# Cross attention and FFN on one core: beginning a pair's accumulator one pair earlier, and moving the last token tile of z behind the FFN's second inner product

## The chip, the core and the metric

The kernel runs on one core of a Trainium2 chip. The metric is the device time of one execution in microseconds (us). The engines are TensorE (PE; PEld is its weight load, which runs beside the matmuls), VectorE (DVE), ScalarE (ACT), GpSimd (POOL) and SyncE (SP, which here only issues DMAs). Matrix products accumulate in PSUM, which has eight banks of 512 f32 per partition.

## The reference, cut to what matters

```python
def fake_quant(x, scale, zp):
    q = jnp.clip(jnp.round(x / s + z), 0., 255.)
    return (q - z) * s

# x: (2, 1024, 2048), ctx: (2, 2048, 2048), all f32
x = x + matmul(fake_quant(layernorm(x), s1, z1), fake_quant(ctx, s2, z2))
z = layernorm(x)
x = x + z @ kernel + bias
      + einsum("bor,btr->bto", B_eff, einsum("bri,bti->btr", A_eff, z))   # gated LoRA
      + einsum("or,btr->bto", B_shared, einsum("ri,bti->btr", A_shared, z))
```

There are two batches of 1024 tokens. A_eff and B_eff are sums over 16 LoRAs of rank 32, weighted by the gates.

## The kernel before

**Cross attention.** The layer-normed x is rounded to uint8 and centred to bf16 integers, eight token tiles of 128 for each batch. A tile (class XTile, L366 to L434) takes statistics on VectorE (L383), a square root on ScalarE (L341), factors on VectorE (up to L402), the rounded row (L409, on ScalarE for all of batch 1), two halves of centring with a sum on ScalarE (L412), two times eight transposes on TensorE (L423) into PSUM, the copy into c1T (L428) and the row's zero point term r_s (L432). Two tiles are a group g = 0..3. The context is quantised by ScalarE (L458) and centred by VectorE (L464), in column blocks n = 0..3 of 512, two of which are held at a time. For each block, `column_term` adds up the columns on TensorE (pcp, L486), copies (L499), takes the mean (pc, L505) and makes the column's zero point term `colt[n]` (L511).

The product of a group and a column block is a `Pair`: a PSUM accumulator `pa` of two banks, one for each token tile j, from three rotating tags. `begin(j)` (L526, ScalarE) writes colt + r_s into half j; `products` (L530) adds 16 matmuls of 128x512 in bf16 to a half; `end` (L547, VectorE) adds the scaled accumulator to y, the running output in SBUF; `stats` (L551) takes the statistics of z. Dependences between instructions on PSUM are kept for a whole tile, so both halves of `pa` count as one. `xattn_pair` (L555 to L563) does begin(0), products of half 0, begin(1), products of half 1, and has the begins in high priority.

Batch 0 starts with a list of steps in an order written by hand (`entry`), which does columns 0 and 1 and the pair (2,0) without `xattn_pair`. Batch 1 has its first tiles prepared during the FFN of batch 0; then columns 0 and 1 go by groups, tiles 4 to 7 being prepared among them (`prep_x`, L1039), and columns 2 and 3 go as in batch 0. Beside the pairs run the LoRA steps: weighted sums of A (pg_a, L574), their transposes (pga, L600), and weighted sums of B (pg_b, L574), which are stored to DRAM (bd).

**z.** `prep_z` (L622) normalises a token tile in two halves on VectorE (L628) into a work buffer wk, transposes it in four groups of four (ptz, L632), and ScalarE copies each (L633). `group_z` does it for the two tiles of a group and stores them to DRAM (zs, issued on ScalarE's queue, L639) for the later outer products. `lora_ax` (L642) multiplies z by LoRA-A (px, L648; axT, L656). These run during column 3: z of group g-1 follows the pair (3, g).

**FFN.** The matmul with the kernel matrix uses a two-level scheme of Strassen's kind: 7 outer products (index o), each of 7 inner products (s, chains u, v, w). `product` (L828) is four f32 matmuls of 128x512, each in two passes, for each of two token tiles; `spread` (L852, VectorE) adds an accumulator to the places of y. Sums of operands (`comb`, L771, and `block`, L762) run on VectorE for the weights' side b and on GpSimd for the z side a; the operands are loaded on SP's queue (L746, L752). `Delta` (L658) holds two PSUM banks and in steps after some products adds bias and LoRA-B times axT (pl, L694; L705).

**Order.** All instructions are put in order ahead of time by a scheduler, engine by engine, from the order in which the program emits them, the priorities and its own estimate of when each is ready. Buffers come from pools (`take`, `give`); a buffer taken again waits for its last reader. The z transposes, the transposes of x, the column sums, px and the LoRA sums share PSUM buffers (ps_m). Before the change, the operands of the first outer product and the z tiles were emitted like this (L1103 to L1109):

```python
group_z(b, 3, wk, zqs[3])      # both tiles, then four stores
big.give(wk)
first.block("b21")
first.comb("t2", "b22", "t1", ALU.subtract)
first.comb("s1", "a21", "a22", ALU.add)
first.comb("s2", "s1", "a11", ALU.subtract)
lora_ax(b, 1, [zqs[2], zqs[3]])
```

and then `ffn`, with `delta = Delta(b)` ahead of its loops.

Of the kernel before, what the change touches and what calls it, by code (L numbers as in the profile page):

```python
# [15 lines left out]
ALU = mybir.AluOpType  # L16
# [82 lines left out]
def tile_quant_xattn_then_lora_ffn(  # L99
# [17 lines left out]
    nc = tc.nc  # L117
    B, S, D = x.shape
    KT = D // P
    MT = S // P  # L120
# [6 lines left out]
    GPB = GB // B  # L127
    GT = B * S // GB
    MG = GT // P
# [422 lines left out]
                    st2[:, self.g * MG + j, self.n, :], y[self.g][:, j, ds(self.n * NB, NB)]  # L552
                )

    def xattn_pair(b, n, g, c1T, c2):  # L555
        p = Pair(b, n, g, c1T, c2)
        for j in range(MG):
            with tc.high_priority():
                p.begin(j)
            p.products(j, range(KT))  # L560
        summed = p.end()
        p.stats()
        return summed  # L563
# [289 lines left out]
            if done:  # L853
                nc.scalar.dma_start(out=out[b, ds(g * GT, GT), cols].rearrange("(j p) n -> p j n", p=P), in_=yp)

    def ffn(b, ops, meanwhile):

        delta = Delta(b)
        for o in range(NO):
            nxt = Operands(b, o + 1) if o + 1 < NO else None  # L860
            chains = {}
            for s in range(len(INNER)):
                product(b, o, s, ops, chains)
                if s in OWN:
                    OWN[s](ops)
                if nxt and s in AHEAD:
                    AHEAD[s](nxt)
                spread(b, o, s, chains)
                if s in (1, 4):
                    delta.step()  # L870
                added = line.last
                if nxt:
                    for name in BLOCKS.get(s, ()):
                        nxt.block(name)
                for name in DROP.get(s, ()):
                    ops.drop(name)
                if nxt:
                    for name in BEGIN.get(s, ()):
                        nxt.load(name)
                with tc.issue_after(added):  # L880
                    meanwhile(o, s)
            ops = nxt
# [20 lines left out]
    wk = big.take()  # L903
    c2b = {}
    c2 = {}
# [4 lines left out]
    def close_c2(n):  # L910
        for t in c2b.pop(n):
            big.give(t)
# [107 lines left out]
    for b in range(B):  # L1020
        if b == 0:
            open_c2(0)
            open_c2(1)
            with in_order(mybir.EngineType.DVE, mybir.EngineType.Activation, mybir.EngineType.PE):
                opened, begun = entry()
            next_block(1)
            with tc.issue_after(last_of[mybir.EngineType.DVE]):
                for p in begun.values():
                    p.stats()
        else:  # L1030
            gate_matrix(b)
            opened = xattn_pair(b, 0, 0, c1T, c2[0])
            xattn_pair(b, 0, 1, c1T, c2[0])
            for g in range(2):
                xattn_pair(b, 1, g, c1T, c2[1])
            for g in range(2, GPB):
                for m in range(g * MG, (g + 1) * MG):
                    with tc.issue_after(opened.ins):
                        prep_x(b, m, c1T, wk)  # L1039
                for n in range(2):  # L1040
                    xattn_pair(b, n, g, c1T, c2[n])
                    if g + 1 == GPB:
                        next_block(n)
                        if n == 0:
                            for r in range(NR):
                                quantise(c2[2], r)
                                if r % 4 == 3:
                                    lora_a_step(b, r // 4)
                            column_term(b, 2, c2[2])
        if b == 0:  # L1050
            for pr in range(GPB // 2):
                nc.sync.dma_start(out=acat[:, :, 3 * pr + 1, :], in_=a_sh)
            for bb in range(B):
                for g in range(GPB):
                    nc.sync.dma_start(out=bd[bb][g, 1 - g % 2], in_=b_sh)
        for g in range(GPB):
            if (b, g) != (0, 0):
                xattn_pair(b, 2, g, c1T, c2[2])
            for r in {0: range(3), 1: range(3, 6), 2: range(6, 8), 3: ()}[g]:
                quantise(c2[3], r)  # L1060
            if 1 <= g <= 2:
                lora_a_step(b, g + 1)
            if g == 2:
                column_term(b, 3, c2[3])
        lora_b_step(b, 0)
        close_c2(2)
        bp.give(colt.pop(2))
        first = Operands(b, 0)
        first.load("b11")
        zqs = {}  # L1070
        for g in range(GPB):
            xattn_pair(b, 3, g, c1T, c2[3])
            big.give(c1T_bufs[g])
            if g == 0:
                first.block("b11")
                first.load("b12")
            elif g == 1:
                first.block("b12")
                first.comb("t1", "b12", "b11", ALU.subtract)
            elif g == 2:  # L1080
                first.load("b22")
            if g < 3:
                lora_b_step(b, g + 1)
            if g > 0:
                zqs[g - 1] = [lit.take() for _ in range(4)]
                group_z(b, g - 1, wk, zqs[g - 1])
            if g == 2:

                lora_ax(b, 0, [zqs[0], zqs[1]])
                for i in range(2):  # L1090
                    for j in range(2):
                        to = lit.take() if i == 0 else zqs[i][j]
                        nc.vector.tensor_add(to, zqs[i][j], zqs[i][2 + j])
                        first.t[f"a{i + 1}{j + 1}"] = to
                for t in (*zqs[0], *zqs[1][2:]):
                    lit.give(t)
        close_c2(3)
        bp.give(colt.pop(3))
        first.block("b22")
        z3 = [big.take() for _ in range(2)]  # L1100
        zqs[3] = [t[:, :, ds(h * GT, GT)] for t in z3 for h in range(2)]
        first.load("b21")
        group_z(b, 3, wk, zqs[3])  # L1103
        big.give(wk)
        first.block("b21")
        first.comb("t2", "b22", "t1", ALU.subtract)
        first.comb("s1", "a21", "a22", ALU.add)
        first.comb("s2", "s1", "a11", ALU.subtract)
        lora_ax(b, 1, [zqs[2], zqs[3]])  # L1109
        for t in zqs[2]:  # L1110
            lit.give(t)
        for t in z3:
            big.give(t)

        state = {"x": 0}

        def meanwhile(o, s):

            if b + 1 == B:
                return  # L1120
            nb = b + 1
            if o < NO - 1:

                for half, m in LOAD_X.get((o, s), ()):
                    load_x(nb, m, slice(half * H, (half + 1) * H))
                return
            if s == 0:
                open_c2(0)
                state["wk"] = big.take()
                state["c1b"] = []  # L1130
                batch[0] = nb
                load_next()
            else:
                load_next()
            if s == 1:
                state["c1b"].append(big.take())
            if s == 3:
                state["c1b"].append(big.take())
            state["c1T"] = [bf(t, GT) for t in state["c1b"]]
            for half, m in LOAD_X.get((o, s), ()):  # L1140
                load_x(nb, m, slice(half * H, (half + 1) * H))
            if s < 4:
                for r in range(2 * s, 2 * s + 2):
                    quantise(c2[0], r)
            if 1 <= s <= 4:
                prep_x(nb, s - 1, state["c1T"], state["wk"])
            if s == 3:
                column_term(nb, 0, c2[0])
                c2b[1] = [big.take()]
                c2[1] = [bf(c2b[1][0], NB)]  # L1150
            if s == 4:
                for r in range(2):
                    quantise(c2[1], r)
                c2b[1].append(big.take())
                c2[1].append(bf(c2b[1][1], NB))
            if s == 5:
                for r in range(2, 5):
                    quantise(c2[1], r)
            if s == len(INNER) - 1:
                for r in range(5, NR):  # L1160
                    quantise(c2[1], r)
                column_term(nb, 1, c2[1])
                state["c1b"] += [big.take() for _ in range(2)]
                state["c1T"] = [bf(t, GT) for t in state["c1b"]]
                for m in range(4, MT):
                    load_x(nb, m, slice(H, D))

        ffn(b, first, meanwhile)
        if b + 1 < B:
            c1T_bufs, c1T, wk = state["c1b"], state["c1T"], state["wk"]  # L1170

# [52 lines left out]
```

## Time and profile before

| | us |
|---|---|
| median of 3 runs | 1082.38 (1082.28 to 1082.62) |
| the profiled execution, its own time | 1082.56 |
| its span | 1080.8 |
| first z transpose of the last z tile of batch 0 | 195.30 |
| first px matmul of the second half, batch 0 / batch 1 | 202.56 / 729.38 |
| first z transpose of batch 1 | 676.35 |

The span runs from the first to the last instruction of the profiled execution; 1.76 us of its time lie outside. Times in the trace count from the span's start. A line of a timeline has the start, the length, the engine, the line of the code, the operation, output <- inputs by their names with sizes, the number of instructions taken together (x16), and in brackets how long the engine had been idle before, and what released it. Matmuls overlap one another, so their distance from start to start says more than their length: 0.2155 us for one in `products`, 0.429 for one of the two passes of an f32 matmul in the FFN, 0.109 for a z transpose, 0.055 for a transpose of x. "Waits" lists for a line of an engine the instructions it waited for, with total time, number and the longest.

### The profile page before, as it was taken

Reading aid. Unit: us, or ns where it says so; the run is one execution under the profiler, and the core shown is the slowest. Engines: PE = TensorE matmul, PEld = TensorE weight load, DVE = VectorE, ACT = ScalarE, POOL = GpSimd, SP = SyncE. Lnnn points to the kernel's source line nnn. Section 1 sums busy time; section 2 is a strip of 40 time slices with the busy share of each in tenths; the row PEclk is TensorE's granted clock in tenths of the full one; section 3 lists DMA queues with packets and bytes.
Section 4 is the critical chain, followed back from the end, with each engine's and each line's share of the span. In section 5 each row is a group of like instructions: output and inputs, shape, how many; then the busy total and the mean of one; then the engine's idle time right before and its main releaser. Section 6 shows DMA issues by size and latency. Waiting matters only on the chain.

```text
span 1080.8 us, 10609 instructions
## 1 busy us (share of the span) xinstructions
PE 1054.6 (98%) x3932; PEld 489.8 (45%) x3932; DVE 766.6 (71%) x949; ACT 247.4 (23%) x351; POOL 253.8 (23%) x104
## 2 busy tenths in 40 slices
PE   5999999999999999999999999999999999999998
PEld 2443345544444444444444444554444444444443
DVE  7986867578877676677859655674969667756851
ACT  5866133210000000001675741331000000000000
POOL 0000003032435302533000000032244531253600
PEclk9999999999999999999999999999999999999999
DMA  9979645788798476699673292559889874748611
GB/s 341 381 196 308 190 176 190 256 316 295 263 339 324 160 264 217 191 372 321 230 246 119 98 266 103 198 210 360 294 269 297 288 269 148 264 146 301 214 39 58
DMA packets 119228, 257.15 MB, mean 238 GB/s; under 512 B 11272, under 2 KB 15496, under 8 KB 118152
## 3 DMA queue, kind: packets, MB, share of 16 engines
q1 hardware_dynamic: 98688, 215.05, 58.4%
q10 hardware_dynamic: 20168, 40.38, 10.7%
q0 software_dynamic: 320, 1.05, 0.4%
q8 instruction: 31, 0.51, 0.2%
q14 instruction: 21, 0.17, 0.1%
HBM read 220.79 MB, written 37.75 MB: 239 GB/s over the span
## 4 chain that ended last, share of the span: by engine, by line
PE 83%; DVE 8%; DMA 4%; ACT 3%; issue 1%; SPq 0%; ACTq 0%
PE fu L828 34%; PE fv L828 17%; PE pa L530 12%; PE fw L828 9%; PE pl L694 3%; PE px L648 3%; PE ptz L632 2%; DMA lit<-in_ctx_dram 2%; DVE st L551 2%; DVE st L383 1%; ACT q2b L458 1%; DVE y L547 1%; ACT big L412 1%; DVE big L771 1%; PE pg_b L574 1%
## 5 line engine op out<-in xcount | busy, mean ns | idle before, releaser
L828 PE MATMUL fu<-big,lit 128*128 128x512 f32 x896 | 395.3, 593 | 0.0
L828 PEld LDWEIGHTS fu<-big,lit 128*128 128x128 f32 x896 | 168.6, 190 | 206.3 <-issue 204.9
L530 PE MATMUL pa<-big,big 128*128 128x512 bf16 x1024 | 237.1, 381 | 7.3 <-ACT pa L526 3.4
L771 POOL TENSOR_TENSOR lit<-lit,lit 128x1024 f32<-128x1024 f32 x56 | 164.7, 2950 | 189.7 <-PE fw L828 74.6
L828 PE MATMUL fv<-big,lit 128*128 128x512 f32 x448 | 197.9, 594 | 0.0
L771 DVE TENSOR_TENSOR big<-big,big 128x2048 f32<-128x2048 f32 x56 | 164.4, 2935 | 0.7
L530 PEld LDWEIGHTS <-big 128*128 128x128 bf16 x1024 | 97.1, 98 | 136.3 <-issue 29.6
L762 POOL TENSOR_TENSOR lit<-lit,lit 128x1024 f32<-128x1024 f32 x32 | 85.7, 2677 | 256.4 <-DMA lit<-zs 230.4
L852 DVE TENSOR_TENSOR y<-y,fu 128x1024 f32<-128x1024 f32 x92 | 108.5, 1215 | 40.6 <-PE fu L828 40.2
L828 PEld LDWEIGHTS fv<-big,lit 128*128 128x128 f32 x448 | 84.3, 190 | 105.0 <-issue 104.7
L458 ACT ACTIVATE q2b<-lit,sc,inv 128x1024 int16<-128x1024 f32 x64 | 76.4, 1232 | 163.7 <-DMA lit<-in_ctx_dram 147.1
L852 DVE TENSOR_TENSOR y<-y,fv 128x1024 f32<-128x1024 f32 x48 | 56.8, 1218 | 78.8 <-PE fv L828 78.8
L762 DVE TENSOR_TENSOR big<-big,big 128x2048 f32<-128x2048 f32 x40 | 101.8, 2546 | 0.0
L828 PE MATMUL fw<-big,lit 128*128 128x512 f32 x224 | 99.4, 592 | 0.0
L683 ACT COPY pl<-bias 128x1024 f32<-128x1024 f32 x16 | 16.3, 1018 | 294.1 <-DVE y L705 258.1
L679 POOL DMA_DIRECT2D bp<-bd x4 | 2.6, 660 | 344.3 <-DMA bd<-q2b 166.3
L852 DVE TENSOR_TENSOR y<-y,fw 128x1024 f32<-128x1024 f32 x24 | 28.4, 1218 | 53.9 <-PE fw L828 53.9
L828 PEld LDWEIGHTS fw<-big,lit 128*128 128x128 f32 x224 | 42.1, 190 | 50.7 <-issue 50.7
L547 DVE SCALAR_TENSOR_TENSOR y<-pa,k_s,y 128x1024 f32<-128x1024 f32 x32 | 41.0, 1280 | 32.2 <-PE pa L530 32.1
L526 ACT ACTIVATE pa<-bp,r_s 128x512 f32<-128x512 f32 x58 | 39.0, 685 | 87.0 <-PE pa L530 57.1
L705 DVE TENSOR_TENSOR y<-pl,y 128x512 f32<-128x512 f32 x64 | 39.8, 679 | 17.5 <-PE pl L694 17.2
L383 DVE BATCH_NORM_STATS2 st<-y 128x6 f32<-128x512 f32 x64 | 41.4, 679 | 5.7 <-DMA y<-in_x_dram 5.6
(93 smaller groups left out, 629.6 us busy)
## 6 DMA issues: line engine op xcount, KB each, us to landing
big<-in_w_dram SPq DMA_DIRECT2D x96, 1024.0 KB
lit<-zs SPq DMA_DIRECT2D x80, 512.0 KB
lit<-in_ctx_dram SPq DMA_DIRECT2D x64, 512.0 KB
out_dram<-y ACTq DMA_DIRECT2D x30, 512.0 KB
zs<-lit ACTq DMA_DIRECT2D x24, 512.0 KB
lit<-in_lora_a_dram SPq DMA_DIRECT2D x32, 256.0 KB
lit<-in_lora_bt_dram SPq DMA_DIRECT2D x32, 256.0 KB
y<-in_x_dram SPq DMA_DIRECT2D x16, 512.0 KB
```

The costliest lines, as they stand in the source:

```text
L383: nc.vector.bn_stats(st1[:, self.m, n, :], self.y[:, ds(n * NB, NB)])
L458: nc.scalar.activation(qi, t, AF.Relu, bias=z2, scale=inv2)
L526: nc.scalar.activation(self.pa[:, j, :], colt[self.n], AF.Identity, bias=r_s[:, m : m + 1])
L530: nc.tensor.matmul(self.pa[:, j, :], self.c1T[:, k, ds(j * P, P)], self.c2[k // 8][:, k % 8, :], start=not self.begun[j], stop=(k == KT - ...
L547: return nc.vector.scalar_tensor_tensor(yp, self.pa, s12, yp, ALU.mult, ALU.add)
L648: nc.tensor.matmul(px[i * 2 * R : (i + 1) * 2 * R, :], acat[:, k, ds(3 * pr + i, 2), :].rearrange("p s r -> p (s r)"), zqs[i][k // KQ][:, ...
L694: nc.tensor.matmul(pl[j][i][:, half], axT[rows, pr, ds(j * P, P)], bt[rows, half], start=False, stop=True, skip_group_check=True,)
L705: line(nc.vector.tensor_add(yb, pl[j][i], yb))
L762: line(eng.tensor_tensor(got[0], got[0], got[1], ALU.add if terms[1][2] > 0 else ALU.subtract))
L771: line(eng.tensor_tensor(out_t, at[p], at[q], op))
L828: nc.tensor.matmul(ps[m], at[:, k, ds(m * P, P)], bt[:, k, :], start=(opens and k == 0), stop=(ends and k == KQ - 1), skip_group_check=True,)
L852: line(nc.vector.tensor_tensor(yp, yp, whole[chain], op))
```

## The change

`xattn_pair` takes the next pair as `then`. It begins both halves of the next pair, in high priority, ahead of the present pair's products, and a pair that is not yet begun has both halves begun in front of its products. In columns 2 and 3 the next pair is given; for the four calls of batch 1's columns 0 and 1 it isn't. The loads of the first outer product's operands move: b11 and b12 ahead of the loop over column 3, b22 and b21 in its first two rounds, and the sum t1 into its third. The last token tile of z (`MT - 1`), the stores of its group, the second `lora_ax` and the construction of `Delta` move into `ffn`, behind the products (0,0) and (0,1), which are emitted together.

```diff
-    def xattn_pair(b, n, g, c1T, c2):
-        p = Pair(b, n, g, c1T, c2)
+    ready = {}
+
+    def begin_pair(b, n, g, c1T, c2):
+        p = ready[b, n, g] = Pair(b, n, g, c1T, c2)
+        with tc.high_priority():
+            for j in range(MG):
+                p.begin(j)
+
+    def xattn_pair(b, n, g, c1T, c2, then=None):
+        if (b, n, g) not in ready:
+            begin_pair(b, n, g, c1T, c2)
+        p = ready.pop((b, n, g))
+        if then:
+            begin_pair(b, *then)
         for j in range(MG):
-            with tc.high_priority():
-                p.begin(j)
             p.products(j, range(KT))
...
-    def ffn(b, ops, meanwhile):
-
-        delta = Delta(b)
+    def ffn(b, ops, meanwhile, last_z):
+
         for o in range(NO):
...
             for s in range(len(INNER)):
-                product(b, o, s, ops, chains)
+                if (o, s) != (0, 1):
+                    product(b, o, s, ops, chains)
+                if (o, s) == (0, 0):
+                    product(b, o, 1, ops, chains)
+                    last_z()
+                    delta = Delta(b)
...
-                xattn_pair(b, 2, g, c1T, c2[2])
+                xattn_pair(b, 2, g, c1T, c2[2], (2, g + 1, c1T, c2[2]) if g + 1 < GPB else (3, 0, c1T, c2[3]))
...
-        first.load("b11")
+        for name in ("b11", "b12"):
+            first.load(name)
+            first.block(name)
...
-            xattn_pair(b, 3, g, c1T, c2[3])
+            xattn_pair(b, 3, g, c1T, c2[3], (3, g + 1, c1T, c2[3]) if g + 1 < GPB else None)
             big.give(c1T_bufs[g])
-            if g == 0:
-                first.block("b11")
-                first.load("b12")
-            elif g == 1:
-                first.block("b12")
-                first.comb("t1", "b12", "b11", ALU.subtract)
-            elif g == 2:
-                first.load("b22")
+            if g < 2:
+                name = ("b22", "b21")[g]
+                first.load(name)
+                first.block(name)
...
+                first.comb("t1", "b12", "b11", ALU.subtract)
...
-        first.block("b22")
...
-        first.load("b21")
-        group_z(b, 3, wk, zqs[3])
-        big.give(wk)
-        first.block("b21")
+        for j in range(MG - 1):
+            prep_z(b, 3 * MG + j, zqs[3], wk)
         first.comb("t2", "b22", "t1", ALU.subtract)
         first.comb("s1", "a21", "a22", ALU.add)
         first.comb("s2", "s1", "a11", ALU.subtract)
-        lora_ax(b, 1, [zqs[2], zqs[3]])
...
+        def last_z():
+
+            prep_z(b, MT - 1, zqs[3], wk)
+            big.give(wk)
+            for q in range(4):
+                nc.scalar.dma_start(out=zs[b][3][q], in_=zqs[3][q])
+            lora_ax(b, 1, [zqs[2], zqs[3]])
+            for t in zqs[2]:
+                lit.give(t)
+            for t in z3:
+                big.give(t)
```

More of the change, by code (lines that the diff above doesn't have):

```diff
@@ L1108, in tile_quant_xattn_then_lora_ffn @@
         first.comb("s2", "s1", "a11", ALU.subtract)
-        lora_ax(b, 1, [zqs[2], zqs[3]])
[L1110 to L1113, printed above, removed]
+        def last_z():
[8 more added lines that the diff above has]
+                big.give(t)
         state = {"x": 0}
@@ L1166, in meanwhile @@
                     load_x(nb, m, slice(H, D))
-        ffn(b, first, meanwhile)
+        ffn(b, first, meanwhile, last_z)
         if b + 1 < B:
```

## The prediction

> **What bounds the kernel now.** I read the shares of engines first, then the slices with the clock, then the waits of TensorE, then the timelines of TensorE and ScalarE around the places that the diff touches.
>
> ```profile
> span 1080.8 us, 10609 instructions
> PE 1054.6 (98%) x3932; PEld 489.8 (45%) x3932; DVE 766.6 (71%) x949; ACT 247.4 (23%) x351; POOL 253.8 (23%) x104
> PEclk9999999999999999999999999999999999999999
> PE 83%; DVE 8%; DMA 4%; ACT 3%; issue 1%; SPq 0%; ACTq 0%
> ```
>
> TensorE is busy for 98% of the span, and the chain that ended last runs on it for 83%. So an edit is worth what it opens or closes of TensorE's own gaps, and nothing else. Next the gaps:
>
> ```profile
> PE pt L423 <- ACT big L412: 9.6, 3, 8.0
> PE pa L530 <- ACT pa L526: 3.4, 5, 1.4
> PE pa L530 <- DVE big L428: 2.6, 2, 2.2
> PE ptz L632 <- DVE big L628: 2.0, 2, 1.7
> ```
>
> Columns: total us, number, longest. The second line is what the new begins of the pairs aim at: 3.4 us. The fourth is the last z tiles: 2.0 us. Of the first, 8.0 is the entry of batch 0, which isn't changed. Measured as lost cadence (start to start, against 0.2155 us of a product in the cross attention, 0.429 of a pass in the FFN, 0.109 of a z transpose) the same places come out at 3.54 in batch 0 (1.52, 0.81, 0.27, 0.94), 0.61 in batch 1 (0.22 at 619.9, 0.39 at 630.8), and 1.88 + 0.27 (batch 0) and 0.40 (batch 1) for z. So 6.7 us is all that the change can win.
>
> **Part 1: both begins ahead of the pair before, batch 0, columns 2 and 3.** TensorE, then ScalarE:
>
> ```profile
> 97.75 3.62 PE L530 MATMUL pa<-big,big 128*128 128x512 bf16 x16
> 102.73 3.61 PE L530 MATMUL pa<-big,big 128*128 128x512 bf16 x16 [1.36 <-ACT pa L526]
> ...
> 99.73 2.37 ACT L458 ACTIVATE q2b<-lit,sc,inv 128x1024 int16<-128x1024 f32 x2 [3.04 <-DMA lit<-in_ctx_dram]
> 102.01 1.28 ACT L526 ACTIVATE pa<-bp,r_s 128x512 f32<-128x512 f32 x2
> ...
> 124.03 0.69 ACT L526 ACTIVATE pa<-bp,r_s 128x512 f32<-128x512 f32 x1 [8.16 <-PE pa L530]
> ```
>
> The first gap isn't made by the order of begins: the begin is queued behind two quantisations that wait for a DMA and end at 102.1. In the static order of the changed kernel they still stand ahead of it, and then come (2,1) half 0, (2,2) half 0, (2,1) half 1. The accumulator is one tile to the scheduler, so the first product now waits for both halves: 102.1 + 3 x 0.6 = 103.9. TensorE is through with pair (2,0) at 101.2, and only half of a LoRA-A sum (0.87 + two format changes of 0.09) goes ahead: 102.15, so a wait of 1.75. That sum is now two halves of 0.87 instead of one (its four matmuls run side by side, two cost the same): +1.06. Later begins are early: their ScalarE time of 0.64 to 0.69 lies under 7 us of products of the pair in front (the 8.16 us of idle time above show the room). Two LoRA-B sums become neighbours, -0.19. Together 1.75 + 1.06 - 0.19 - 3.54 = **-0.9**. If the cover were gone, each begin would cost 0.7 again.
>
> **Part 2: the last z tile behind product (0,1).** The tile moves its statistics (0.4), two normalisations, four groups of four transposes, four copies, four stores on ScalarE's queue, then the 64 small matmuls of LoRA-A times x (7.0), bias loads and Delta's steps. All is still issued; TensorE's sum of work is the same.
>
> ```profile
> 195.30 1.06 PE L632 MATMUL ptz<-ident,big 128*128 128x128 f32 x8 [1.72 <-DVE big L628]
> ```
>
> This wait goes, since its normalisation no longer stands in front of product (0,1)'s end. What is late next, by the static order: the second last tile's transposes behind VectorE's y sum, aggregates and the comb t1 of 2.28 (0.45); ScalarE's four copies of tile 5 behind a square root that waits for VectorE's aggregates (1.15); the last tile behind two adds of fw of 1.2 each (0.5 to 1.0, taken 0.75); and 0.75 of small losses between tiles 0 and 1 and the products. I walked the stage with row durations from the end of pair (3,1) and its LoRA-B sum to the first px matmul, less the FFN products that now run in front of it: 54.5. Before, the same stretch is 147.8 to 202.56 = 54.76, so **-0.25** in batch 0. In batch 1 it is 53.2, with hardly a wait, so the same walk makes **+1.3**. On the queues: loads b12 and b21 are issued earlier on SP, each behind the release of a c1T buffer, and are wanted only by t1 and t4; the stores of z issue on ScalarE later, and are read by o = 1, after 50 us of products. I cost both at nothing; if a store were late by its own landing, SP's loads behind it would wait, but not TensorE.
>
> VectorE's normalisation takes 0.81 alone, but 1.65 beside POOL's sums of L771 (183.0), and L771 on VectorE 4.14 against 2.28. The moved tile could meet those: 0.84 for each half at worst, +1.7 in each batch. I take nothing, as POOL's next sums start behind fw. [...]
>
> **Part 3: batch 1's first columns.** Here the helper is called without a following pair, and yet it changes: both begins now stand ahead of the products instead of one before each half, and the scheduler orders anew.
>
> ```profile
> 567.85 17.15 PE L530 MATMUL pa<-big,big 128*128 128x512 bf16 x78
> 585.02 0.62 PE L423 MATMUL pt<-ident_h,big 128*128 128x128 bf16 x8
> 586.15 0.62 PE L423 MATMUL pt<-ident_h,big 128*128 128x128 bf16 x8 [0.51 <-ACT big L412]
> 586.72 4.48 PE L530 MATMUL pa<-big,big 128*128 128x512 bf16 x20
> 591.10 0.62 PE L423 MATMUL pt<-ident_h,big 128*128 128x128 bf16 x8
> ...
> 583.72 1.15 ACT L412 ACTIVATE big<-big,n_centre 128x1024 bf16<-128x1024 uint8 x1
> 586.61 2.08 ACT L409 ACTIVATE big<-y,ox,kx 128x2048 uint8<-128x2048 f32 x1
> ```
>
> Before, products (x20, x3, x34) lie between the transposes of tiles 4, 5 and 6, and cover ScalarE's 4.4 us of rounding (L409 2.08) and centring (2 x 1.14) of each tile. In the changed order TensorE has four pairs, then the transposes of tiles 4, 5 and 6 back to back, then pair (0,2). ScalarE has tile 4, two begins, L409 of tiles 5 and 6, and only then the centring of 5 and 6. First arrival: the column sums of column 1 have no products between them any more and wait for VectorE's last centrings (558.8 on): about 1.65 later, less small waits, +1.3, so 589.8 at tile 4's transposes. ScalarE: tile 4 is centred at 586.2, begins to 587.7, two L409 to 591.85, centring of 5 to 594.2, of 6 to 596.65; the last transposes and VectorE's copy, and pair (0,2) starts at 597.4. Its work in front would have been done at 589.8 + 6 x 0.48 = 592.7. So **4.7** us of waiting in place of 0.7 (0.51 and some 0.2 before). The begin waits at 619.9 and 630.8 go (-0.6), a new one at pair (2,0) comes (+0.4). Sum 1.3 + 4.7 - 0.7 - 0.6 + 0.4 = **+5.1**. Bounds of the 4.7: nothing, if ScalarE is ahead by the two L409, to 6.9, if VectorE's copies of 0.65 and the sum r_s 0.27 (L428, L432) close each tile in turn.
>
> A longer wait may cost more than itself. At the entry TensorE waits 8.01 us; the eight transposes behind it take 1.03 instead of 0.62, and the four products at 18.93 take 1.74, though the granted clock reads 1.00 in those windows. Up to 20.5 that is about 2.4 us too many. The waits here are cut by transposes into pieces of 3.1 at most, and behind the 2.22 us wait at 16.39 I can't tell old slowness from new; I take nothing, and keep 2.4 as the other end. [...]
>
> **Sum.** -0.9 - 0.25 + 1.3 + 5.1 = +5.25. The profiled execution took 1082.56 (span 1080.8 and 1.76 around it), 0.18 above the median of 1082.38. 1082.56 + 5.25 = 1087.8; less 0.18, the forecast is **1087.6**. A measurement of this kernel can tell 0.2% (2.2 us) from no change, so this is slower by 0.5%.
>
> **Rivals.**
> 1. *The transposes do not wait (not slower).* Place: tiles 5 and 6 of batch 1. It needs ScalarE to have both L409 done by the time TensorE reads tile 4, 589.8, so tile 4 centred at 584.0 and not 586.2, or TensorE later by 4 us for another reason. For it: VectorE's factors of tile 4 leave ScalarE idle for 1.44 before 581.6. Against it: before, the order was closer and tile 5 still came at 589.8. Without the 4.7: 1082.9, no change.
> 2. *Only the gains.* As 1, and the new waits in z don't come either (the normalisation is early behind so many products): 1082.38 - 3.5 + 1.8 - 0.6 - 2.15 - 0.4 + 0.4 = 1077.9. Against it is the batch-1 stretch, which has no z wait to win but 0.4.
> 3. *More late than I count.* The transposes wait 6.9, z meets POOL in both batches (3.4 at worst, half of it likely) and a slow spell of 2.4: up to 1087.6 + 2.2 + 1.7 + 1.2 = 1092.7.
> 4. *The begins gain nothing*, because the scheduler orders them behind waits as before: part 1 is 0 instead of -0.9: 1088.5, inside the forecast's own band.
>
> **Chances.** Forecast with rival 4 (1085 to 1090.5) 0.52; rival 3 0.16; rival 1 (1080.2 to 1084.5) 0.20; rival 2 0.12. Faster by over 0.2% is rival 2, 0.12; within is rival 1, 0.20; slower is the rest, 0.68. The range leaves out most of rival 2 and the end of rival 3: 1080.0 to 1092.0.
>
> **What would show it.** After the change, "pt waiting for ACT L412" should be some 4 us longer than now, with three tiles' transposes back to back near 590 and pair (0,2) of batch 1 at about 597. "pa waiting for ACT L526" should shrink to about 2, all of it near 102 to 104. The 1.72 at z's last tile is gone, with pieces of 0.5 to 1.2 at ScalarE's copies in both batches. The first px of the second half starts at about 203.3 in batch 0 with two FFN matmuls more behind it. I am wrong if TensorE's products still lie between the transposes of tiles 4 to 6, or if batch 1 reaches its first z transpose (676.35 now) less than 3 us later.

## The result, and the profile after

The changed kernel takes 1098.67 us (median of 4 runs, 1097.0 to 1100.6), the kernel before 1082.5 in the runs beside it: 1.015 times as long, 95% interval 1.0132 to 1.0167, or 16 us slower. The forecast was 1087.6, its range ended at 1092.0. The direction was right, the size was not. The profiled execution of the changed kernel took 1100.6, its span 1098.8; the page of that execution:

```profile
span 1098.8 us, 10575 instructions
...
PE 1059.5 (96%) x3903; PEld 495.1 (45%) x3932; DVE 775.0 (71%) x949; ACT 247.9 (23%) x351; POOL 246.0 (22%) x104
...
PEclk9999999999999999999998999999999999999999
```

TensorE is still the bound, at 96% and no longer 98%, and one slice shows a granted clock below nine tenths, where before had none. 29 matmul records are missing in this trace (3903 of 3932). From the list of TensorE's waits (total us, number, longest):

```profile
PE pt L423 <- ACT big L412: 13.6, 5, 8.0
PE ptz L642 <- DVE big L638: 5.9, 2, 3.0
PE pg_a L584 <- DMA lit<-in_lora_a_dram: 3.5, 1, 3.5
...
PE pa L530 <- ACT pa L526: 2.0, 2, 1.5
...
PE pcp L486 <- DVE big L428: 1.0, 1, 1.0
```

Lines of the code are shifted by ten (L632 is L642, L628 is L638, L574 is L584). The waits for a begin fell from 3.4 to 2.0, as the change meant. But z's transposes wait 5.9 in place of 2.0, tiles 4 to 6 add 4, and a wait for a LoRA-A load is new. With landmarks on TensorE the 18.0 us between the two spans fall as follows. A z stage runs from its first transpose to the first px matmul of its second half; the four passes of the FFN, 0.43 each, that run inside it only after the change are counted with the FFN. The forecast's terms stand beside the differences:

| stretch | before, us | after, us | difference | forecast |
|---|---|---|---|---|
| start to batch 0's first z transpose | 147.8 | 147.0 | -0.8 | -0.9 |
| z stage of batch 0 | 54.7 | 57.9 | +3.2 | -0.25 |
| FFN to batch 1's first transpose | 328.6 | 328.6 | 0 | 0 |
| batch 1's transposes, to the last of tile 7 | 77.4 | 83.3 | +5.9 | +5.3 |
| from there to batch 1's first z transpose | 67.9 | 74.1 | +6.2 | -0.2 |
| z stage of batch 1 | 53.0 | 56.5 | +3.5 | +1.3 |
| rest | 351.4 | 351.4 | 0 | 0 |

(The forecast's +5.1 for batch 1 is split here: 1.3 + 4.7 - 0.7 up to the transposes, -0.6 + 0.4 behind.) The first z transpose of batch 1 starts at 676.43 in the trace before (the 676.35 given above is a little early) and at 690.89 in the changed kernel. Of the five stretches with a term in the forecast, two came out as forecast and three did not. Here is what is seen in them.

**z.** VectorE, and below it GpSimd, in the z stage of batch 0 of the changed kernel (start, length, engine, line):

```profile
181.41 0.28 DVE L347 RECIPROCAL r_z<-sd_z 128x1 f32<-128x1 f32 x3
181.60 2.53 DVE L349 SCALAR_TENSOR_TENSOR nt_z<-ve_z,r_z 128x1 f32<-128x1 f32 x2
184.05 0.14 DVE L350 TENSOR_SCALAR nt_z<-nt_z 128x1 f32<-128x1 f32 x1
184.12 2.31 DVE L349 SCALAR_TENSOR_TENSOR nt_z<-ve_z,r_z 128x1 f32<-128x1 f32 x1
186.35 0.15 DVE L358 TENSOR_TENSOR rstd_z<-r_z,nt_z 128x1 f32<-128x1 f32 x1
186.42 0.20 DVE L350 TENSOR_SCALAR nt_z<-nt_z 128x1 f32<-128x1 f32 x2
186.59 2.20 DVE L358 TENSOR_TENSOR rstd_z<-r_z,nt_z 128x1 f32<-128x1 f32 x2
188.72 0.80 DVE L638 TENSOR_SCALAR big<-y,mv_z,rstd_z 128x1024 f32<-128x1024 f32 x1
...
181.63 7.08 POOL L781 TENSOR_TENSOR lit<-lit,lit 128x1024 f32<-128x1024 f32 x3 [10.85 <-DVE r_z L347]
```

An instruction on one element per partition takes 0.2 us elsewhere; here three of them take 2.1 to 2.4 (one of the two in each of the rows of 2.53 and 2.20, and the one of 2.31), which is one GpSimd sum each (7.08 / 3 = 2.36). While GpSimd works through s1, s2 and s3, VectorE gets an instruction with two tensors through only between two sums (the one of 0.15 at 186.35). The last small one ends at 188.79; in the run hold below, where GpSimd stands still, it ends at 182.41, 6.4 us earlier. TensorE's transposes wait for the normalisation behind it:

```profile
189.67 1.94 PE L642 MATMUL ptz<-ident,big 128*128 128x128 f32 x8 [2.97 <-DVE big L638]
191.40 1.77 PE L838 MATMUL fw<-big,lit 128*128 128x512 f32 x2
```

These eight transposes take 1.94, others 1.04: the cadence behind the wait is halved.

**Tiles 4 to 6.** TensorE and ScalarE of the changed kernel near 590:

```profile
592.15 1.06 PE L423 MATMUL pt<-ident_h,big 128*128 128x128 bf16 x16
597.38 2.17 PE L423 MATMUL pt<-ident_h,big 128*128 128x128 bf16 x16 [4.17 <-ACT big L412]
599.81 1.03 PE L423 MATMUL pt<-ident_h,big 128*128 128x128 bf16 x8 [0.26 <-ACT big L412]
...
590.89 1.30 ACT L526 ACTIVATE pa<-bp,r_s 128x512 f32<-128x512 f32 x2 [0.37 <-DVE ox L402]
592.13 4.07 ACT L409 ACTIVATE big<-y,ox,kx 128x2048 uint8<-128x2048 f32 x2
```

This is the pile-up of the forecast: no products between the tiles, two begins and two L409 ahead of tile 5's centring. Again the transposes behind the wait run at half cadence.

**The LoRA-A load.** TensorE, then SP's issue:

```profile
639.59 1.54 PE L584 MATMUL pg_a<-lit,gmat 128*32 128x512 f32 x8 [3.55 <-DMA lit<-in_lora_a_dram]
...
633.95 4.16 SPq L216 DMA_DIRECT2D lit<-in_lora_a_dram  x4
```

The scheduler drew the sum pg_a of block 2 ahead of pair (2,1)'s first product, to fill the wait for its begins. In batch 0 the data is there. In batch 1 its load is issued at 633.95, the last of its four parts ends its issue at 638.11, and TensorE comes to the sum at 636.04. Before, the sum ran later in its pair, 10 us after the last part was issued, and did not wait:

```profile
637.10 1.07 PE L574 MATMUL pg_a<-lit,gmat 128*32 128x512 f32 x8
...
622.23 4.62 SPq L216 DMA_DIRECT2D lit<-in_lora_a_dram  x4
```

**The clock.** Windows of the changed kernel (from:to, length, busy time of PE, PEld, DVE, ACT, POOL with the number of instructions, granted clock, share of the DMA engines, GB/s):

```profile
186.00:189.00 3.00, 0.70 (x2) 0.00 (x0) 3.00 (x7) 0.51 (x2) 2.71 (x2) 1.00 0.82 307
189.00:192.00 3.00, 2.33 (x9) 2.10 (x10) 3.00 (x4) 0.94 (x2) 0.00 (x0) 0.58 0.11 42
...
597.00:603.00 6.00, 4.95 (x35) 3.64 (x37) 3.60 (x10) 5.72 (x12) 0.00 (x0) 0.54 0.01 3
...
640.00:644.00 4.00, 4.00 (x17) 1.11 (x10) 2.54 (x5) 1.63 (x2) 0.00 (x0) 0.57 1.06 286
```

Behind three of the four waits of 2.9 us and more the granted clock is 0.54 to 0.58 in these windows. Taken more closely it reads 0.51 over 189.4 to 192.9, over 595.6 to 602.5 and over 640.0 to 643.5. Behind the fourth, 2.94 us in batch 1's z, it reads 1.00.

### The profile page after: what moved, and what is told of

The parts are those of the page before. It is cut to its first block, busy times and chain, and to the rows that moved or that the text cites. A ratio compares the mean times of both kernels' runs of the same rounds, so it can differ in the third digit from the quotient of the medians.

```text
span 1098.8 us, 10575 instructions
## 1 busy us (share of the span) xinstructions
PE 1059.5 (96%) x3903; PEld 495.1 (45%) x3932; DVE 775.0 (71%) x949; ACT 247.9 (23%) x351; POOL 246.0 (22%) x104
## 4 chain that ended last, share of the span: by engine, by line
PE 84%; DVE 8%; DMA 4%; ACT 2%; issue 1%; SPq 0%; ACTq 0%
PE fu L838 34%; PE fv L838 17%; PE pa L530 14%; PE fw L838 9%; PE pl L704 3%; PE ptz L642 3%; DVE st L383 2%; PE px L658 2%; DMA lit<-in_lora_a_dram 1%; DMA y<-in_x_dram 1%; DVE nt_z L349 1%; PE pt L423 1%; DMA out_dram<-y 1%; ACT big L412 1%; PE pg_b L584 1%
## 5 line engine op out<-in xcount | busy, mean ns | idle before, releaser
L530 PE MATMUL pa<-big,big 128*128 128x512 bf16 x995 | 231.5, 383 | 7.3 <-DVE big L428 2.6
L781 POOL TENSOR_TENSOR lit<-lit,lit 128x1024 f32<-128x1024 f32 x56 | 161.4, 2891 | 192.5 <-PE fw L838 68.3
L772 POOL TENSOR_TENSOR lit<-lit,lit 128x1024 f32<-128x1024 f32 x32 | 81.5, 2546 | 263.0 <-DMA lit<-zs 228.7
```

Of the source, the lines that this page charges most:

```text
L530: nc.tensor.matmul(self.pa[:, j, :], self.c1T[:, k, ds(j * P, P)], self.c2[k // 8][:, k % 8, :], start=not self.begun[j], stop=(k == KT - ...
L772: line(eng.tensor_tensor(got[0], got[0], got[1], ALU.add if terms[1][2] > 0 else ALU.subtract))
L781: line(eng.tensor_tensor(out_t, at[p], at[q], op))
```

## The experiments

Differences in us to before, from each run's own profiled execution, by the stretches of the table above; the clock is the mean granted over that execution. It is no price: in ptr and z_hold much of what it lacks is at the entry (0.53 and 0.51 over 7.2 to 21.0), where the reading of before is 1.00 and its rows are nearly the same.

| run | median | ratio, 95% interval | start | z 0 | transposes | to z 1 | z 1 | clock |
|---|---|---|---|---|---|---|---|---|
| the change | 1098.67 | 1.0132 to 1.0167 | -0.8 | +3.2 | +5.9 | +6.2 | +3.5 | 0.993 |
| z_only | 1095.33 | 1.0099 to 1.0130 | -0.3 | +6.6 | +1.2 | +0.8 | +5.8 | 0.995 |
| pairs_only | 1096.50 | 1.0111 to 1.0141 | -1.2 | +2.8 | +4.8 | +3.5 | +2.9 | 0.996 |
| old_first | 1095.10 | 1.0093 to 1.0125 | -1.2 | +3.3 | +0.5 | +6.2 | +3.5 | 0.996 |
| ptr | 1096.68 | 1.0105 to 1.0139 | -1.5 | +2.0 | +6.5 | +3.8 | +3.8 | 0.988 |
| hold | 1093.88 | 1.0073 to 1.0104 | -0.9 | 0.0 | +5.4 | +5.7 | +1.8 | 0.995 |
| lora | 1097.23 | 1.0117 to 1.0143 | -1.3 | +3.3 | +5.6 | +2.0 | +5.1 | 0.993 |
| mended | 1086.35 | 1.0019 to 1.0042 | -1.5 | 0.0 | +0.6 | +0.7 | +1.8 | 0.999 |
| z_hold | 1083.02 | 0.9989 to 1.0007 | +1.0 | -1.1 | 0.0 | 0.0 | +0.9 | 0.994 |
| before_hold | 1079.96 | 0.9964 to 0.9983 | -0.1 | -2.2 | +0.1 | 0.0 | -0.4 | 1.000 |
| mended2 | 1091.37 | 1.0069 to 1.0098 | -1.6 | +2.8 | 0.0 | +0.1 | +3.7 | 0.995 |
| mended3 | 1081.63 | 0.9972 to 1.0005 | -1.5 | -1.5 | 0.0 | +0.1 | +0.3 | 0.999 |
| best | 1080.10 | 0.9950 to 0.9976 | -1.7 | -2.3 | +0.8 | +0.9 | -1.1 | 1.000 |

What the columns lack of a span's difference lies in the FFN: 1.9 and 1.8 in mended2, 0.8 in pairs_only and in best, nothing elsewhere.

**Each part alone.** z_only is the change with the old `xattn_pair`; pairs_only is the kernel before with the new one and its calls.

```diff
-            xattn_pair(b, 3, g, c1T, c2[3], (3, g + 1, c1T, c2[3]) if g + 1 < GPB else None)    # z_only
+            xattn_pair(b, 3, g, c1T, c2[3])
...
-            xattn_pair(b, 3, g, c1T, c2[3])                                                     # pairs_only
+            xattn_pair(b, 3, g, c1T, c2[3], (3, g + 1, c1T, c2[3]) if g + 1 < GPB else None)
```

> The changed kernel with the pairs as before (begin of half 0, its products, begin of half 1, its products; no pair begun early), so only the moved z tile and the moved loads remain. Theory A (the 16 us come from two places: batch 1's first columns, whose transposes and LoRA-A load are late, +12, and the z stage, where VectorE's small two-input instructions each wait for a GpSimd sum, +3.2 in batch 0 and +3.5 in batch 1): 1082.5 + 6.7 = 1089, range 1087 to 1091, with the waits of 3 us on L638's normalisation in both batches. Theory B (the z stage costs little by itself and is only pushed by what the early begins do to ScalarE and VectorE): 1082 to 1084.

> The kernel before with only the pairs changed (both halves begun ahead, the next pair begun during the one in front); z, loads and FFN as before. Theory A: batch 0 gains about 1.2, batch 1's first columns lose 12: 1082.5 + 11 = 1093, range 1091 to 1096. Theory B (pairs lose only what the transposes wait, 4 to 5, and the rest of the 16 needs both parts): 1086 to 1088.

Both were 3 to 6 us worse than theory A said, and both rivals fell too. The parts don't add: 14.0 and 13.6 us of span alone, 18.0 together. In z_only the z stages lose more than in the full change: in batch 0 TensorE waits 5.3 for a normalisation, in batch 1 two normalisations take 5.68 in place of 1.6.

```profile
186.07 1.94 PE L632 MATMUL ptz<-ident,big 128*128 128x128 f32 x8 [5.27 <-DVE big L628]
...
716.28 5.68 DVE L628 TENSOR_SCALAR big<-y,mv_z,rstd_z 128x1024 f32<-128x1024 f32 x2
```

Even pairs_only, which touches nothing in z, loses 2.8 and 2.9 there. What they share is that GpSimd's three sums fall beside the statistics and the normalisations, and the runs ptr and hold below go after that.

**Batch 1's first columns.**

```diff
-            opened = xattn_pair(b, 0, 0, c1T, c2[0])
+            opened = halves_pair(b, 0, 0, c1T, c2[0])    # begin, products, begin, products
```

and so for the other three calls of batch 1's columns 0 and 1.

> The changed kernel, but the four calls for batch 1's columns 0 and 1 begin half by half as before; early begins in columns 2 and 3 and the moved z tile stay. Theory A: TensorE's order in batch 1's first columns is that of before again, the 12 us there go: 1098.7 - 12 = 1087, range 1085 to 1089, with no wait for LoRA-A's load. Theory B (the early begins of columns 2 and 3 and their queueing make batch 1 late): above 1094.

The stretch to tile 7 is back to +0.5, so 5.4 of the 5.9 there are the two begins ahead of the products, as forecast. But the next stretch keeps its +6.2, with a 5.0 us wait for the LoRA-A load: theory A was wrong to see that wait as a consequence of the transposes. It comes with the early begins of column 2, and z_only, which has none, doesn't have it. By its time (1095.10) the run is theory B's.

```profile
PE pg_a L594 <- DMA lit<-in_lora_a_dram: 5.0, 1, 5.0
```

Nor is it enough to say that the load is issued late. Here its four parts are issued from 624.91 to 629.64, less than 3 us later than before, and the sum still can't start until 634.16. It was drawn ahead to a place where its data had not landed; before, it ran at 637.10.

**The small instructions.**

```diff
-        nc.vector.scalar_tensor_tensor(t, ve, r0, r0, ALU.mult, ALU.mult)
+        (nc.vector.tensor_scalar if name[0] == "z" else nc.vector.scalar_tensor_tensor)(t, ve, r0, r0, ALU.mult, ALU.mult)
...
-        nc.vector.tensor_mul(rstd, r0, t)
+        nc.vector.tensor_scalar(rstd, r0, t, None, ALU.mult)
```

> The changed kernel, with two small instructions of z's norm on VectorE (128x1 elements; L349 and L358 of the norm) put as a tensor_scalar whose factors are per-partition scalars, so that each reads one tensor and not two; the values and TensorE's order are the same. Theory A (a VectorE instruction with two SBUF tensors waits for a whole GpSimd sum of 2.3 us, five of them in a row): they take 0.2 instead of 2.2 to 2.5, the waits of 3 us on L638 go and with them the slow cadence behind: 3 to 4.5 in each batch, so 1091, range 1089 to 1093. Theory C (VectorE is late by its own queue, sums and combs): the waits stay, 1097 to 1100.

Only 2.0 us off, with intervals that overlap those of the change, so theory A missed its size, and 1096.68 lies just under theory C's 1097 to 1100. The timeline of VectorE says why:

```profile
180.29 0.45 DVE L349 TENSOR_SCALAR nt_z<-ve_z,r_z 128x1 f32<-128x1 f32 x2
...
180.72 0.26 DVE L349 TENSOR_SCALAR nt_z<-ve_z,r_z 128x1 f32<-128x1 f32 x1
180.90 0.20 DVE L358 TENSOR_SCALAR rstd_z<-r_z,nt_z 128x1 f32<-128x1 f32 x1
...
181.14 5.20 DVE L638 TENSOR_SCALAR big<-y,mv_z,rstd_z 128x1024 f32<-128x1024 f32 x2
```

The small ones take 0.2 beside GpSimd (its sums run from 180.67), as theory A says of an instruction with one tensor, and the waits of 3 us are gone (the longest left for L638 is 1.4). But the delay moves on to the two normalisations, 5.20 instead of 1.5. So it isn't the instruction that has to change, but the meeting.

**Moving GpSimd's sums.**

```diff
-        first.comb("s1", "a21", "a22", ALU.add)
-        first.comb("s2", "s1", "a11", ALU.subtract)
...
+            added = first.comb("s1", "a21", "a22", ALU.add)     # at the end of last_z, s2 behind it
+            tc.add_manual_dep(added.ins, normed[b, MT - 2].ins.name, <wait for its end>, reason="hold")
```

(`normed` holds the last normalisation of each tile; what stands in angle brackets is shortened.)

> The changed kernel with GpSimd's first sum of the z stage (s1, and so s2 and s3 behind it on the same queue) made to wait for the last normalisation of the second last z tile; the order on TensorE, VectorE and ScalarE is unchanged, only the time at which GpSimd works moves. Theory A (VectorE's instructions that read two SBUF tensors, and its normalisations, wait for whole GpSimd sums): the small instructions take 0.2 again, the 3.1 us waits of the z transposes go in both batches with the slow cadence behind one of them: 3.2 + 3.5 off, 1092, range 1090 to 1094. Theory C (VectorE is late by the length of its own queue): no gain, 1097 to 1100, or slower as s2 comes later.

The order on TensorE, VectorE, ScalarE and GpSimd is that of the change, instruction by instruction, and z falls from +3.2 to 0.0 in batch 0 and from +3.5 to +1.8 in batch 1; 4.8 us off in the median, 1093.88, inside theory A's range. VectorE in this run, at the same instructions:

```profile
181.28 0.28 DVE L347 RECIPROCAL r_z<-sd_z 128x1 f32<-128x1 f32 x3
181.47 0.35 DVE L349 SCALAR_TENSOR_TENSOR nt_z<-ve_z,r_z 128x1 f32<-128x1 f32 x2
...
181.80 0.21 DVE L349 SCALAR_TENSOR_TENSOR nt_z<-ve_z,r_z 128x1 f32<-128x1 f32 x1
...
182.18 0.23 DVE L358 TENSOR_TENSOR rstd_z<-r_z,nt_z 128x1 f32<-128x1 f32 x2
...
197.51 2.96 DVE L640 TENSOR_SCALAR big<-y,mv_z,rstd_z 128x1024 f32<-128x1024 f32 x1
...
190.17 9.75 POOL L783 TENSOR_TENSOR lit<-lit,lit 128x1024 f32<-128x1024 f32 x4 [19.72 <-DVE big L640]
```

The same two-tensor instructions take 0.2 when GpSimd stands still. Theory C is out. The normalisation of 2.96 is what is left: it now meets s4, the last of the four sums, and TensorE waits 1.5 in each batch.

**The LoRA-A sums.** They are queued behind the 16th product of the pair in front of them in the program.

```diff
-                lora_a_step(b, g + 1)
+                with tc.issue_after(halfway[b, 2, g].ins):
+                    lora_a_step(b, g + 1)
```

> The changed kernel with the LoRA-A sums of column blocks 2 and 3 queued on TensorE behind the first half of the pair they follow in the program, so that they no longer go ahead of it. Theory A (the sum pg_a of block 2 was drawn ahead of pair (2,1) as filler, and in batch 1 meets a load that isn't there: 3.7 us, and a slow cadence behind it): 4 to 5 off, 1094, range 1092 to 1096. Theory D (the load itself is late, as ScalarE's quantising of the context runs late, and whoever comes next waits as long): 1097 to 1099.

The wait for the load is gone, so theory D is out, and the stretch falls from +6.2 to +2.0, so 4.1 of it are shown in the trace. The median doesn't show it: it falls by 1.4, the intervals overlap, and 1097.23 would be theory D's time. Part of the gain is lost again in z of batch 1, where this execution had a slow spell that the changed kernel's had not (+5.1 against +3.5), and the four runs spread over 3 us. In the 2.0 that stay is a wait of 1.0 for a begin, up to 636.37.

**Together.** mended has the edits of old_first, hold and lora:

```diff
+            opened = halves_pair(b, 0, 0, c1T, c2[0])
...
+            tc.add_manual_dep(added.ins, normed[b, MT - 2].ins.name, <wait for its end>, reason="hold")
...
+                with tc.issue_after(halfway[b, 2, g].ins):
```

> The changed kernel with three repairs together: half by half begins in batch 1's columns 0 and 1, GpSimd's sums held back in the z stage, LoRA-A sums behind the first half of their pair. Theory A (these three make up the whole of the loss): the span of the first of them alone was 12.4 above before, of which 6.8 in z and 6.8 in batch 1; both go, the gain of 1.2 in batch 0 stays: 1082, range 1079.5 to 1084. Theory E (a wait that is hidden behind these comes up in their place): 1086 or more.

Stretch by stretch the repairs take most of the loss away, but theory A's 1082 is missed, and the median, 1086.35, is in theory E's range. The profiled execution is the fastest of the eight (1084.26), and its stretches account for 1.7 us above before: 1.8 in z of batch 1, where s4 meets the last normalisation, +0.6 and +0.7 ahead of it, and -1.5 at the start, although pair (2,1) waits 2.8 there behind four begins in a row on ScalarE. What makes the median 2.1 us longer than that execution isn't shown.

The z part alone, and then the kernel before, each with the sums held until the last normalisation:

```diff
-        first.comb("s1", "a21", "a22", ALU.add)
+        added = first.comb("s1", "a21", "a22", ALU.add)
+        tc.add_manual_dep(added.ins, normed[b, MT - 1].ins.name, <wait for its end>, reason="hold")    # before_hold; in z_hold at the end of last_z
```

> The moved z tile and loads alone (pairs as before), with GpSimd's sums s1, s2, s3 held until the last normalisation of the last z tile; the order on TensorE, VectorE and ScalarE is that of the run with the z part alone, which took 1095.3 and lost 6.6 and 5.8 in the two z stages. Theory A (all of that is VectorE waiting for GpSimd): both go, 1095.3 - 12 = 1083.5, range 1081.5 to 1086. Theory C (the move itself makes VectorE late): 1090 or more.

12.3 us off z_only with the same order on every engine, and level with before. So the loss of the z part against before was this meeting.

> The kernel before, unchanged but for GpSimd's sums of the z stage, which wait for the last normalisation of z; orders on all other engines are those of before. Theory A: before too pays for GpSimd there (the comb of 4.14 instead of 2.28, a normalisation of 1.65 instead of 0.8, and then the last z tile's transposes 1.9 late in batch 0, 0.4 in batch 1): 1 to 2 off, 1081.3, range 1080 to 1082.5. Rival: VectorE was not what the last tile waited for, no change, 1082.5 to 1083.5.

2.9 us off a kernel in which the order on every engine stayed the same, as theory A said and a little more (1079.96, its range ended at 1080). Before had the same meeting in a milder form, in its normalisation of 1.65 and its comb of 4.14 (here 0.80 and 2.23):

```profile
183.00 1.65 DVE L628 TENSOR_SCALAR big<-y,mv_z,rstd_z 128x1024 f32<-128x1024 f32 x1
...
184.86 4.14 DVE L771 TENSOR_TENSOR big<-big,big 128x2048 f32<-128x2048 f32 x1
...
178.96 7.90 POOL L771 TENSOR_TENSOR lit<-lit,lit 128x1024 f32<-128x1024 f32 x3 [10.72 <-DMA zs<-lit]
```

GpSimd in before_hold, then TensorE's last z tile:

```profile
196.75 9.44 POOL L773 TENSOR_TENSOR lit<-lit,lit 128x1024 f32<-128x1024 f32 x4 [28.64 <-DVE big L630]
...
192.98 1.04 PE L634 MATMUL ptz<-ident,big 128*128 128x128 f32 x8
```

The last tile comes at 192.98 without a wait, in before at 195.30 after 1.72.

The two runs also price the move itself. With the sums held in both, the kernel with the moved tile and loads takes 1083.02 (0.9989 to 1.0007 of before) and the one without 1079.96 (0.9964 to 0.9983): with GpSimd out of VectorE's way the move costs 3.1 us (0.5 of it, in batch 1, a wait of TensorE for a held sum). Of the 3.4 between their profiled executions, 2.4 lie in the two z stages and 1.1 in the start.

**Two more tries at the whole change.** mended2 begins pair (2,1) half by half and holds the sums until the last tile's normalisation (`MT - 1`); mended3 holds s1 to s3 as mended does, and s4 until the last one. best is before_hold with mended2's pairs and places of the LoRA-A sums. The condition on g is written out here to be read:

```diff
-                xattn_pair(b, 2, g, c1T, c2[2], (2, g + 1, c1T, c2[2]) if g + 1 < GPB else (3, 0, c1T, c2[3]))
+                if g == 1: halves_pair(b, 2, 1, c1T, c2[2])
+                else: xattn_pair(b, 2, g, c1T, c2[2], None if g == 0 else (2, 3, c1T, c2[2]) if g == 2 else (3, 0, c1T, c2[3]))
...
-            p.comb("s4", "a12", "s2", ALU.subtract, place="a12"),
+            hold(p.b, p.o, p.comb("s4", "a12", "s2", ALU.subtract, place="a12")),               # mended3
```

> As the run with three repairs (1086.35, its profiled execution 1084.26), with the sums held until the last tile's normalisation instead of the second last's (there the last normalisation still met a sum and the last transposes waited 1.6 in both batches), and with pair (2,1) begun half by half and not ahead, so that its first product waits for one begin (2.9 us at 100.5, 1.1 at 625). Theory A: 3.3 and 2.5 off, the slow spells with them: 1080.5, range 1078.5 to 1082.5, which would be below before. Theory E: another wait takes their place, 1084 or more.

A miss on theory A, and inside theory E's range: product (0,2) needs s2, and waits for it in both batches. The line of TensorE's waits:

```profile
PE fu L857 <- POOL lit L798: 6.3, 2, 3.1
```

> All parts of the change kept but those that lose: batch 1's columns 0 and 1 and pair (2,1) begun half by half, LoRA-A sums behind the first half of their pair, GpSimd's s1 to s3 held until the second last z tile is normalised, and s4 until the last one is. In the last run the sums held until the last tile came too late for product (0,2), which waited 3.3 us in both batches; in the one before it s4 ran into the last normalisation (2.98 instead of 0.81) and its transposes waited 1.6. Theory A: s1 to s3 fit between the two tiles, neither wait comes: 1080, range 1078.5 to 1082, with 1.5 won at the pairs of batch 0. Theory E: another wait takes their place, 1084 or more.

Held: 1081.63, not told from before (the interval takes in 1); its twelve runs lie between 1080.0 and 1086.5. Its profiled execution, the fastest, wins 1.5 at the begins and 1.5 in batch 0's z. The second is the hold's and not the change's: before_hold alone wins 2.2 there.

> The kernel before with the GpSimd sums of z held until its last normalisation (1079.96 by itself), and with the early begins of columns 2 and 3 from pair (2,2) on, LoRA-A sums behind the first half of their pair; z, loads and FFN as before. Theory A: 1.2 to 1.5 more off at the pairs of batch 0, none in batch 1: 1078.5, range 1077.5 to 1080.5. Rival: the new order makes z's stage late as in the run with the pairs alone (there 2.8 and 2.9), 1081 or more.

1080.10, 0.9963 of before: inside the range, but as fast as before_hold alone. In the profiled executions it wins 1.5 more than before_hold at the pairs of batch 0 and 0.7 in z of batch 1, and gives 0.7, 0.9 and 0.8 back in batch 1 and the FFN.

## Why the prediction was wrong

**Part 1, batch 0's pairs (-0.9): right.** -0.8 in the changed kernel; the first wait is 1.5, up to 104.33, behind half of the LoRA-A sum, as forecast.

**Part 3, tiles 4 to 6 (+5.3 up to tile 7): right in place and order, 0.6 short.** The wait was 4.2 in one piece (forecast 4.7, cut into pieces of 3.1 at most); ScalarE's order was as read. The forecast took nothing for a slow clock and kept 2.4 as the other end: the clock reads 0.51 over 595.6 to 602.5, from the middle of the wait on, and 32 transposes come every 0.107 us instead of 0.056, an estimated 1.6 us at most, since some of it would have been waits for the centring. So the nearness of 5.3 and 5.9 is in part luck: a wait put 0.5 too long stands against a slow clock put at nothing. In the changed kernel the clock reads 0.51 behind the waits of 2.97, 4.17 and 3.55 us, and 1.00 behind that of 2.94. The rival "the transposes do not wait" is out.

**Part 2, z (-0.25 and +1.3): wrong, +3.2 and +3.5.** The step that failed: "The moved tile could meet those: 0.84 for each half at worst [...] I take nothing, as POOL's next sums start behind fw." That was wrong twice. GpSimd's first sums start when VectorE has made a21 and a22, at 181.6, and not behind fw, so all three run beside the statistics of tiles 5 to 7. And the price was read off one normalisation (1.65) that met the end of a sum. The row beside it, the comb of 4.14 instead of 2.28, showed a wait of 1.9, nearly a whole sum; taken for the three two-tensor instructions that waited, it gives an estimated 5.6 us (measured: 6.4 until the last of them). The walk's other terms were about 1 us too high: in mended3, where the small instructions and the last normalisation meet no sum, the stages come out at -1.5 and +0.3. Beside GpSimd sums of 2.36 us each the runs show 2.1 to 2.4 us for 128x1 instructions with two inputs and up to 2.98 for a normalisation (0.81 alone), and 0.2 for the small ones where there is no sum or only one tensor. How one engine holds up the other isn't shown.

**Batch 1 behind the transposes (-0.2): wrong, +6.2.** The step was "only half of a LoRA-A sum goes ahead", counted for batch 0 alone. The same move of pg_a in batch 1 was in the static order, but the prediction didn't ask when its data land: they were put at nothing, and the sum waited 3.5 us for them, with a slow clock behind. lora shows 4.1 of it.

**Part 2's queues at nothing: right.** TensorE waits for none of the moved loads or stores in the changed kernel.

Rival 3 named GpSimd and a slow clock as what could be more, but priced them at 1.7 and 1.2 and didn't see the LoRA-A load.

What stays open: why a wait of 2.94 us is followed by a slow spell in one run and not in the next (batch 1's z: not in the changed kernel, but in lora). No experiment took the clock by itself. Why best loses 0.8 and 0.9 in batch 1 was not tried, nor where the move's 3.1 us with held sums come from. 2.0 of the +6.2 are only seen as waits in the trace.

## What to carry to other kernels

Before pricing a move on VectorE, lay GpSimd's timeline beside it: here a VectorE instruction with two tensors in SBUF, even of 128x1 (2.1 to 2.4 us in place of 0.2), or an f32 normalisation (up to 2.98 in place of 0.81), that fell into a GpSimd sum of 2.36 cost the rest of that sum, and a chain of three small ones cost 6.4 us, nearly a sum each. Where a scheduler draws work forward to fill a gap, look up when that work's data land, in each batch by itself. And holding the off-path engine back until the critical chain is through can be worth more than moving the chain: one added wait gave 2.9 us here, and no part of the change gave anything measurable on top of it (1080.10 against 1079.96).

## What the runs showed of the hardware that was not expected

- Beside a GpSimd sum of two SBUF tensors (128x1024, 2.36 us), VectorE's 128x1 instructions with two SBUF tensors took 2.1 to 2.4 us, and f32 normalisations (tensor_scalar, 128x1024) up to 2.98; 128x1 tensor_scalars with per-partition factors, reciprocals (0.15 at 186.50 in ptr), and (in mended) y sums with one input in PSUM, 1.2 each, did not wait.
- GpSimd's sums get longer too, when VectorE's instruction is a long one. Three sums took 7.08 beside the small instructions, 7.90 in before, and 9.47 in pairs_only beside a VectorE sum of 128x2048 that took 4.29 instead of 2.28:

```profile
717.55 4.29 DVE L781 TENSOR_TENSOR big<-big,big 128x2048 f32<-128x2048 f32 x1
...
717.34 9.47 POOL L781 TENSOR_TENSOR lit<-lit,lit 128x1024 f32<-128x1024 f32 x3 [8.89 <-PE px L658]
```

- Of 17 waits of TensorE of 2.9 us and more behind the entry, in all these traces, 15 were followed within 8 us by a granted clock of half (it reads 0.51 in the windows above), for 3.5 or 6.9 us at a time; of those of 1 to 2.9 us only three (ending in ptr at 558.68 and 595.29, in lora at 595.25). Half of the low time behind a wait, an estimated 1.6 to 3.0 us (189.67 to 192.9 in the changed kernel, 202.66 to 208.6 in mended2), is what it can cost where TensorE is the bound. In hold the runs of 1090.1 and 1090.4 had a mean granted clock of 0.998, and those of 1093.7 to 1094.8 had 0.991 to 0.995.
- The reading of the clock may miss a slow spell. At the entry eight transposes take 1.03 us instead of 0.62 both in before, where it reads 1.00, and in z_hold, where it reads 0.51 over 7.2 to 21.0; that the clock was halved in before too isn't shown.
